# A causal mask that moves from a TensorE product to a VectorE addition, in a reordered attention pipeline

## Chip, cores and metric

The kernel runs on one core of a Trainium2 chip. The metric is the device time of one execution in microseconds, and the time of a kernel is the median over its runs. The engines are TensorE (PE in the profile; PEld is its weight load), VectorE (DVE), ScalarE (ACT), GpSimd (POOL) and SyncE (SP, which here only issues DMAs). Each engine works through its own instructions in program order and waits on semaphores for the others.

## What is computed

One transformer block on x of 8 sequences x 256 tokens x 256 features, all in float32. The change touches the attention scores; the rest is given for orientation.

```python
x = x + layernorm(attention(layernorm(x)))
x = x + layernorm(moe(layernorm(x)))

def attention(x):                       # 16 query heads, 4 key/value heads, D = 128
    q, k, v = split(x @ w_qkv.T)
    q, k = rope(layernorm(q, qn_g, qn_b)), rope(layernorm(k, kn_g, kn_b))
    scores = q @ k.T / sqrt(128)
    scores = where(causal, -inf, scores)          # no key later than its query
    return softmax(scores) @ v @ w_o.T

# moe: 8 experts of width 176, the two best per token, and a shared expert of width 352
```

## The kernel before

The program has three stretches. First comes a start of some 30 us, in which weights and x arrive, the weights are centred (so that the layer norm over a head needs no mean) and the first projections are made; its steps stand in the program one by one, in an order written out by hand. Then comes a software pipeline of slots, one slot for each of the 8 x 12 attention units plus some for filling and draining. The last stretch, from about 600 us on, computes the experts by blocks of tokens, and does not change.

A sequence has two tiles of 128 tokens (t = 0, 1). A projection `(g, t)` yields 512 columns for one tile: g = 0 to 3 are four query heads each, 4 is the keys of the four heads, 5 is the values. A unit `(g, t, r0)` is a piece of attention for key/value head g: for t = 0 four heads with 128 keys in one unit, for t = 1 two heads with 256 keys in each of two units. [...] A sequence so has 12 projections and 12 units.

In slot s the loop calls each step once, for the unit or projection that is at that step: `multiply(s)` makes a projection, `square`, `deviation` and `power` its norm's scale (ScalarE, VectorE, POOL), `normalise(s-1)` applies it on ScalarE, `rope_cos(s-1)` and `rope_sin(s-1)` turn it on VectorE and POOL, `rope_sum(s-2)` adds, `turn_heads(s-2)` transposes on TensorE and `settle_heads(s-2)` adds the rope of the norm's offset out of PSUM. With u = s - 7, `score(u)`, `maximum(u)` and `exponential(u)` make the exponentials, `inverse(u-1)` and `weights(u-1)` divide by the sums, `turn_weights(u-2)`, `copy_weights(u-2)` and `value(u-2)` multiply with the values, and `copy_value(u-3)` stores. `outputs` multiplies with `w_o`. Steps that come once per tile (`residual`, `inner`, `turn_inner`, `route`, `rank`, `mark`, `enter` and others, started by `ends`; `prepare`, `prepared`, `turn_x`, started by `begins` at a given place of the 12) are spread over the slots. The order of the calls in the slot is the order of each engine's instructions; no scheduler changes it.

PSUM is shared by tags: `mm` (projections) two buffers, `tr` (every transpose, and the small products of route, rank and enter) two, `sc` two, `av` and `o` one each. A step that needs a buffer waits for the last reader of the tile that had it.

The mask is a bfloat16 tile with -1e30 above the diagonal and 0 elsewhere. It is added by TensorE: `score` issues a product of a bfloat16 identity `identb` with the mask into the scores' own 128-key block, and the float32 score products of that block accumulate onto it. `identb` is a copy of the float32 identity, made by VectorE at the start. In the start, `find(g)` sums a group of weights on VectorE, `centre(g)` or `centre_on_act(g)` subtracts the mean on VectorE or ScalarE, `tables(s, engine)` builds the rope tables with the norm's gains on the engine named, `gains` spreads the gains over the partitions and `turn_offsets` transposes the offsets' tables.

Of the kernel before, what the change touches and what calls it, by code (L numbers as in the profile page):

```python
# [19 lines left out]
P = 128  # L20
# [28 lines left out]
def block_kernel(  # L49
# [92 lines left out]
    for j, w in enumerate((wg, wu)):  # L142
# [14 lines left out]
    nhalf = const.tile([P, REP], F32, name="nhalf")  # L157
    nc.gpsimd.memset(nhalf, -0.5)

    identb = const.tile([P, P], BF16, name="identb")  # L160
    mask = const.tile([P, REP, P], BF16, name="mask")
    nc.gpsimd.memset(mask, 0.0)
    nc.gpsimd.affine_select(
        out=mask,
# [1 line left out]
        compare_op=ALU.is_ge,  # L166
        fill=NEG,
        base=0,
        pattern=[[0, REP], [-1, P]],
        channel_multiplier=1,  # L170
    )
    iota_e = const.tile([P, E], F32, name="iota_e")
# [56 lines left out]
    def find(g):  # L229


        heads = w_qkv[g].rearrange("p c (h d) -> p (c h) d", d=D)
        wm = small.tile([P, KC * REP], F32, tag="wm", name=f"wm_{g}")
        nc.vector.tensor_reduce(out=wm, in_=heads, axis=AX.X, op=ALU.add)
        nc.vector.tensor_scalar_mul(wm, wm, -1.0 / D)
        found[g] = heads, wm
# [130 lines left out]
    with ExitStack() as actx:  # L367
# [152 lines left out]
        def gains():  # L520

            nc.vector.tensor_scalar_mul(gb_row[:, 2:], gb_row[:, 2:], scale)
            gbp = ps_o.tile([P, 4, D], F32, tag="o", name="gbp")
            nc.tensor.matmul(
                gbp.rearrange("p n d -> p (n d)"), lhsT=ones_row,
                rhs=gb_row.rearrange("p n d -> p (n d)"), start=True, stop=True,
            )
            nc.scalar.copy(gb_all, gbp)
# [10 lines left out]
        def score(b, u):  # L539
            g, t, r0 = units[u]  # L540
            nh, w = shape(u)
            sc = ps_sc.tile([P, nh, w], F32, tag="sc", name=f"sc_{b}_{u}")

            def product(h, k, **flags):
                nc.tensor.matmul(  # L545
                    sc[:, h, k * P : (k + 1) * P],
                    lhsT=seqs[b]["qT"][g][:, r0 + h, t * P : (t + 1) * P],
                    rhs=seqs[b]["kT"][:, g, k * P : (k + 1) * P],
                    **flags,
                )  # L550

            if t == 1:
                for h in range(nh):
                    product(h, 0, start=True, stop=True)
            nc.tensor.matmul(  # L555
                sc[:, :, w - P :], lhsT=identb, rhs=mask[:, :nh, :], start=True, stop=False
            )
            for h in range(nh):
                product(h, t, start=False, stop=(h == nh - 1))
            now["sc", b, u] = sc  # L560

        def maximum(b, u):
            nh, w = shape(u)
# [222 lines left out]
        def each(f, k, n=NS):  # L786

            if 0 <= k < B * n:
                f(*divmod(k, n))
# [38 lines left out]
        with tc.manual_schedule():  # L828

            warm = ps_tr.tile([P, 4, P], F32, tag="tr", name="warm")  # L830
            for k in range(WARM):
                nc.tensor.transpose(warm[:, k % 4, :], ident, ident)
            nc.vector.tensor_copy(identb, ident)
            prepare(0, 0)
            gains()
            prepare(0, 1)
            prepared(0, 0)
            find(4)
            turn_x(0, 0)
            centre(4)  # L840
            multiply(0, 0)
            find(0)
            prepared(0, 1)
            tables("k", nc.gpsimd)
            square(0, 0)
            tables("q", nc.vector)
            multiply(0, 1)
            centre_on_act(0)
            square(0, 1)
            deviation(0, 1)  # L850
            multiply(0, 4)
            power(0, 1)
            find(1)
            turn_x(0, 1)
            square(0, 4)
            multiply(0, 2)
            multiply(0, 5)
            normalise(0, 1)
            deviation(0, 4)
            power(0, 4)  # L860
            rope_cos(0, 1)
            rope_sin(0, 1)
            normalise(0, 4)
            square(0, 2)
            rope_cos(0, 4)
            rope_sin(0, 4)
            deviation(0, 2)
            centre_on_act(1)
            turn_offsets("k")
            turn_offsets("q")  # L870
            rope_sum(0, 4)
            rope_sum(0, 1)
            turn_heads(0, 1)
            power(0, 2)
            turn_heads(0, 4)
            multiply(0, 3)
            settle_heads(0, 1)
            normalise(0, 2)
            rope_cos(0, 2)
            square(0, 5)  # L880
            deviation(0, 5)
            rope_sin(0, 2)
            multiply(0, 6)
            power(0, 5)
            settle_heads(0, 4)
            normalise(0, 5)
            square(0, 6)
            square(0, 3)
            rope_sum(0, 2)
            find(2)  # L890
            turn_heads(0, 2)
            settle_heads(0, 2)
            rope_cos(0, 5)
            rope_sin(0, 5)
            deviation(0, 6)
            power(0, 6)
            LAST = B * NS + LAG + 3
            for s in range(FIRST, LAST):
                u, j = s - LAG, s
                each(copy_value, u - 3)  # L900
                ends(s, residual, 5)
                each(inverse, u - 1)
                each(turn_weights, u - 2)
                each(copy_weights, u - 2)
                each(rope_sum, j - 2)
                each(normalise, j - 1)
                each(weights, u - 1)
                begins(s, prepare, 1, 4)
                each(score, u)
                each(maximum, u)  # L910
                park(s)
                each(rope_cos, j - 1)
                each(rope_sin, j - 1)
                each(multiply, j)
                each(turn_heads, j - 2)
                begins(s, prepare, 0, 2)
                ends(s, inner, 6)
                begins(s, turn_x, 0, 6)
                ends(s, route, 8)
                begins(s, turn_x, 1, 7)  # L920
                ends(s, turn_inner, 7)
                each(settle_heads, j - 2)
                ends(s, rank, 9)
                ends(s, gates, 8)
                ends(s, mark, 9)
                ends(s, enter, 10)
                each(square, j)
                each(deviation, j)
                ends(s, shares, 9)
                each(power, j)  # L930
                ends(s, inner_rows, 6)
                ends(s, residual_sum, 5)
                begins(s, prepared, 1, 5)
                each(exponential, u)
                centre_last(s)
                outputs(s)
                begins(s, prepared, 0, 2)
                each(value, u - 2)
                if s == B * NS:

                    wgu_sb = wpool.tile([P, KC, E * 2 * HE], F32, tag="w", name="wgu_sb")
                    for j, w in enumerate((wg, wu)):
                        for c in range(KC):
                            nc.sync.dma_start(
                                out=wgu_sb[:, c, :].rearrange("p (e g h) -> p e g h", g=2, h=HE)[
                                    :, :, j, :
                                ],
                                in_=w[c * P : (c + 1) * P, : E * HE].rearrange(
                                    "p (e h) -> p e h", h=HE
                                ),  # L950
                            )

            z = B - 1
            rank(z - 1, 1)
            mark(z - 1, 1)
            shares(z - 1, 1)
            for o in range(sum(OUTPUTS[: LAST - OUT - z * NS]), H):
                output(z, o)
            enter(z - 1, 1)
            residual(z, 0)  # L960
            residual_sum(z, 0)
            for o in range(H, 2 * H):
                output(z, o)
            inner(z, 0)
            inner_rows(z, 0)
            fill(2)
            turn_inner(z, 0)
            residual(z, 1)
            route(z, 0)
            residual_sum(z, 1)  # L970
            fill(1)
            rank(z, 0)
            inner(z, 1)
            mark(z, 0)
            inner_rows(z, 1)
            fill(2)
            enter(z, 0)
            turn_inner(z, 1)
            route(z, 1)
            fill(1)  # L980
            rank(z, 1)
            mark(z, 1)
            fill(2)
            enter(z, 1)
            for t in range(NT):
                gates(z, t)
            for t in range(NT):
                shares(z, t)
# [425 lines left out]
```

## Time and profile before

| What | Value |
|---|---|
| Median of 3 runs | 768.57 us (767.18 to 769.37) |
| Profiled execution | 768.42 us, span from first to last instruction 766.3 us |
| Mean granted TensorE clock | 0.988 |
| Slots | score products from 28.1 to 563.4 us |
| DMA, page's slices | 316 and 139 GB/s in the first two of 40, about 1 to 9 up to the middle of the slots |
| POOL rope_sin (L481) | 128 + 32 instructions, 0.72 to 1.24 us each |
| ScalarE exponentials (L576) | 256, mean 435 ns |

The page gives each engine's busy time and its share of the span; slices of the span in tenths; the chain of work that ended last; and groups of instructions by line, with tile names, shapes, count, total and mean time, and behind the second bar the time that the engine stood idle just before them and for whom. In timeline lines the first two numbers are start and length in us, and brackets give the wait ahead. [...]

### The profile page before, as it was taken

Reading aid. Unit: us, or ns where it says so; the run is one execution under the profiler, and the core shown is the slowest. Engines: PE = TensorE matmul, PEld = TensorE weight load, DVE = VectorE, ACT = ScalarE, POOL = GpSimd, SP = SyncE. Lnnn points to the kernel's source line nnn. Section 1 sums busy time; section 2 is a strip of 40 time slices with the busy share of each in tenths; the row PEclk is TensorE's granted clock in tenths of the full one; section 3 lists DMA queues with packets and bytes.
Section 4 is the critical chain, followed back from the end, with each engine's and each line's share of the span. In section 5 each row is a group of like instructions: output and inputs, shape, how many; then the busy total and the mean of one; then the engine's idle time right before and its main releaser. Section 6 shows DMA issues by size and latency. Waiting matters only on the chain.

```text
span 766.3 us, 11943 instructions
## 1 busy us (share of the span) xinstructions
PE 736.0 (96%) x3800; PEld 553.1 (72%) x3800; DVE 498.5 (65%) x1372; ACT 458.0 (60%) x1448; POOL 395.0 (52%) x455
## 2 busy tenths in 40 slices
PE   7799999999999999999999999999999899999994
PEld 4457777777777777777777777777887677777774
DVE  7767657677676867776776778567546563353564
ACT  3678877576677757676776777576651333333332
POOL 6656667265555627473654556275312434455423
PEclk9899999999999999999999999999999999999998
DMA  9400000000000000000000000000403133343422
GB/s 316 139 1 1 1 1 9 0 8 2 8 1 9 0 8 8 1 8 0 9 1 8 1 7 4 5 8 23 137 9 89 42 104 111 104 125 104 122 84 75
DMA packets 26917, 32.40 MB, mean 42 GB/s; under 512 B 2980, under 2 KB 23048, under 8 KB 26856
## 3 DMA queue, kind: packets, MB, share of 16 engines
q1 hardware_dynamic: 22752, 21.94, 8.8%
q0 software_dynamic: 3408, 9.31, 4.5%
q8 instruction: 31, 0.51, 0.3%
q10 hardware_dynamic: 696, 0.40, 0.2%
q14 instruction: 30, 0.25, 0.1%
HBM read 22.33 MB, written 9.31 MB: 41 GB/s over the span
## 4 chain that ended last, share of the span: by engine, by line
PE 88%; DVE 4%; ACT 3%; DMA 2%; issue 1%; POOL 1%; DVEq 0%; POOLq 0%; ACTq 0%
PE qkv L413 20%; PE o L644 15%; PE sc L545 11%; PE av L625 10%; PE gu L1167 6%; PE tp L607 5%; PE py L1192 5%; PE tq L508 4%; PE gus L285 4%; PE sd L305 2%; PE sc L555 2%; PE xt L1150 1%; PE ht L1182 1%; PE in L773 1%; DMA w_qkv<-in_wqkvT 1%
## 5 line engine op out<-in xcount | busy, mean ns | idle before, releaser
L413 PE MATMUL qkv<-w_qkv,xnT 128*128 128x512 f32 x384 | 184.5, 604 | 3.7 <-DVE xnT L403 3.1
L481 POOL TENSOR_TENSOR t<-qn,sg_q 128x256 f32<-128x256 f32 x128 | 118.9, 948 | 58.6 <-ACT qn L455 58.6
L446 POOL TENSOR_TENSOR rstds<-ves,nhalf 128x4 f32<-128x4 f32 x80 | 84.7, 1059 | 108.9 <-DVE ves L437 54.2
L644 PE MATMUL o<-wo_sb,oT 128*128 128x256 f32 x512 | 125.1, 384 | 0.0
L545 PE MATMUL sc<-kT,q 128*128 128x128 f32 x768 | 109.4, 277 | 3.5 <-DVE q L518 3.5
L455 ACT ACTIVATE qn<-qkv,rstds 128x128 f32<-128x128 f32 x320 | 91.8, 373 | 31.3 <-POOL rstds L446 30.4
L576 ACT ACTIVATE ex<-sc,nmx 128x128 f32<-128x128 f32 (+1 forms) x256 | 105.5, 435 | 2.2 <-DVE nmx L565 1.8
L413 PEld LDWEIGHTS qkv<-w_qkv,xnT 128*128 128x128 f32 x384 | 66.8, 194 | 54.7 <-issue 48.0
L545 PEld LDWEIGHTS sc<-kT,q 128*128 128x128 f32 x768 | 101.7, 193 | 5.7 <-ACT ex L576 3.7
L625 PE MATMUL av<-pT,v 128*128 128x256 f32 (+1 forms) x320 | 98.5, 422 | 0.2 <-ACT pT L612 0.2
L644 PEld LDWEIGHTS o<-wo_sb,oT 128*128 128x128 f32 x512 | 91.4, 190 | 9.3
L565 DVE TENSOR_REDUCE nmx<-sc 128x2 f32<-128x512 f32 (+1 forms) x96 | 66.2, 690 | 48.8 <-PE sc L545 47.1
L612 ACT COPY pT<-tp 128x512 f32<-128x512 f32 x96 | 57.3, 597 | 26.1 <-PE tp L607 26.1
L508 PEld LDWEIGHTS tq<-ident,t 128*128 128x128 f32 x320 | 39.9, 142 | 43.6 <-issue 37.1
L607 PEld LDWEIGHTS tp<-ident,ex 128*128 128x128 f32 x384 | 47.6, 141 | 24.9 <-ACT sq L431 7.9
L625 PEld LDWEIGHTS av<-pT,v 128*128 128x128 f32 x320 | 59.0, 190 | 8.5 <-issue 1.0
L469 DVE TENSOR_TENSOR t<-qn,cg_q 128x512 f32<-128x512 f32 x64 | 44.6, 697 | 25.0 <-ACT qn L455 24.5
L596 ACT ACTIVATE ex<-ex,rr 128x256 f32<-128x256 f32 x128 | 59.2, 525 | 0.1
L431 ACT ACTIVATE sq<-qkv 128x512 f32<-128x512 f32 x80 | 48.2, 602 | 17.9 <-PE qkv L413 12.3
L607 PE MATMUL tp<-ident,ex 128*128 128x128 f32 x384 | 57.9, 273 | 0.7 <-DVE xnT L403 0.5
L437 DVE TENSOR_REDUCE ves<-sq 128x4 f32<-128x516 f32 x80 | 54.6, 682 | 5.5 <-ACT sq L431 5.5
L1140 POOL DMA_INDIRECT xb<-xf_rows,src x39 | 37.5, 961 | 37.7 <-PE xt L1150 20.7
(202 smaller groups left out, 1216.3 us busy)
## 6 DMA issues: line engine op xcount, KB each, us to landing
ys<-yb SPq DMA_DIRECT2D x39, 128.0 KB
w_qkv<-in_wqkvT SPq DMA_DIRECT2D x6, 512.0 KB
x_all<-in_x SPq DMA_DIRECT2D x8, 256.0 KB
wo_sb<-in_woT SPq DMA_DIRECT2D x1, 2048.0 KB
xf_rows<-xf SPq DMA_DIRECT2D x16, 128.0 KB
out<-yo SPq DMA_DIRECT2D x14, 128.0 KB
wgu_sb<-in_wg SPq DMA_DIRECT2D x2, 704.0 KB
wgu_sb<-in_wu SPq DMA_DIRECT2D x2, 704.0 KB
```

The lines of the kernel that those rows point to most:

```text
L413: nc.tensor.matmul(ps.rearrange("p h d -> p (h d)"), lhsT=seqs[b]["xnT"][t][:, c, :], rhs=w_qkv[g][:, c, :], start=(c == 0), stop=(c == KC ...
L446: nc.gpsimd.tensor_tensor(rstd, now.pop(("ve", b, j)), nhalf, ALU.pow)
L455: nc.scalar.activation(qn[:, h, :], ps[:, h, :], AF.Copy, scale=rstd[:, h : h + 1])
L481: nc.gpsimd.tensor_tensor(t2[:, :, lo : lo + HD], qn[:, :, hi : hi + HD], sg[s][:, t : t + 1, lo : lo + HD].to_broadcast([P, REP, HD]), AL ...
L508: nc.tensor.transpose(tr[:, h, :], t1[:, h, :], ident)
L545: nc.tensor.matmul(sc[:, h, k * P : (k + 1) * P], lhsT=seqs[b]["qT"][g][:, r0 + h, t * P : (t + 1) * P], rhs=seqs[b]["kT"][:, g, k * P : ( ...
L565: nc.vector.tensor_reduce(out=nm, in_=now["sc", b, u], axis=AX.X, op=ALU.max, negate=True)
L576: nc.scalar.activation(ex[:, h, :], sc[:, h, :], AF.Exp, bias=nm[:, h : h + 1], accum_out=rs[:, h : h + 1],)
L596: nc.scalar.activation(ex[:, h, :], ex[:, h, :], AF.Copy, scale=rr[:, h : h + 1])
L607: nc.tensor.transpose(tr[:, c, :], ex[:, h, k * P : (k + 1) * P], ident)
L625: nc.tensor.matmul(now["av"][:, r0 : r0 + nh, :].rearrange("p h q -> p (h q)"), lhsT=seqs[b]["v"][:, k, g * D : (g + 1) * D], rhs=pT[:, k ...
L644: nc.tensor.matmul(now["o", b, t], lhsT=seqs[b]["oT"][h // REP, t][:, h % REP, :], rhs=wo_sb[:, h, :], start=(h == 0), stop=(h == H - 1),)
```

## The change

The product with the identity goes, and `identb` with it. The score products of a unit then stand alone, each with start and stop. A new step `masked(u)` adds the mask to the scores' own block in PSUM, in place, by VectorE; the mask keeps one copy of its 128 x 128 instead of four and is spread over the heads by the access pattern. `masked` is called between `score` and `maximum`. The calls in the slot and the steps of the start stand in another order. In the slot, among others: `park` and `rope_sum` come first, `copy_value` follows `turn_weights`, `normalise` follows `score`, `inverse` comes after `rope_sum`, `square` comes before `turn_heads`, `mark` and `shares` come at the end, `centre_last` ahead of `exponential`, and `turn_x(…, 0)` moves from place 6 to place 7. In the start, both tiles of x are turned before `gains`, `centre(4)` follows `find(0)`, and `tables("q")` follows `find(1)`.

```diff
--- before.py
+++ after.py
@@ -157,8 +157,7 @@
     nhalf = const.tile([P, REP], F32, name="nhalf")
     nc.gpsimd.memset(nhalf, -0.5)
 
-    identb = const.tile([P, P], BF16, name="identb")
-    mask = const.tile([P, REP, P], BF16, name="mask")
+    mask = const.tile([P, P], BF16, name="mask")
     nc.gpsimd.memset(mask, 0.0)
     nc.gpsimd.affine_select(
         out=mask,
@@ -166,7 +165,7 @@
         compare_op=ALU.is_ge,
         fill=NEG,
         base=0,
-        pattern=[[0, REP], [-1, P]],
+        pattern=[[-1, P]],
         channel_multiplier=1,
     )
     iota_e = const.tile([P, E], F32, name="iota_e")
@@ -541,23 +540,21 @@
             nh, w = shape(u)
             sc = ps_sc.tile([P, nh, w], F32, tag="sc", name=f"sc_{b}_{u}")
 
-            def product(h, k, **flags):
-                nc.tensor.matmul(
-                    sc[:, h, k * P : (k + 1) * P],
-                    lhsT=seqs[b]["qT"][g][:, r0 + h, t * P : (t + 1) * P],
-                    rhs=seqs[b]["kT"][:, g, k * P : (k + 1) * P],
-                    **flags,
-                )
-
-            if t == 1:
+            for k in range(t + 1):
                 for h in range(nh):
-                    product(h, 0, start=True, stop=True)
-            nc.tensor.matmul(
-                sc[:, :, w - P :], lhsT=identb, rhs=mask[:, :nh, :], start=True, stop=False
-            )
-            for h in range(nh):
-                product(h, t, start=False, stop=(h == nh - 1))
+                    nc.tensor.matmul(
+                        sc[:, h, k * P : (k + 1) * P],
+                        lhsT=seqs[b]["qT"][g][:, r0 + h, t * P : (t + 1) * P],
+                        rhs=seqs[b]["kT"][:, g, k * P : (k + 1) * P],
+                        start=True,
+                        stop=True,
+                    )
             now["sc", b, u] = sc
+
+        def masked(b, u):
+            nh, w = shape(u)
+            own = now["sc", b, u][:, :, w - P :]
+            nc.vector.tensor_add(own, own, mask[:, None, :].to_broadcast([P, nh, P]))
 
         def maximum(b, u):
             nh, w = shape(u)
@@ -830,112 +827,112 @@
             warm = ps_tr.tile([P, 4, P], F32, tag="tr", name="warm")
             for k in range(WARM):
                 nc.tensor.transpose(warm[:, k % 4, :], ident, ident)
-            nc.vector.tensor_copy(identb, ident)
             prepare(0, 0)
-            gains()
             prepare(0, 1)
             prepared(0, 0)
             find(4)
+            prepared(0, 1)
             turn_x(0, 0)
-            centre(4)
+            turn_x(0, 1)
+            gains()
             multiply(0, 0)
             find(0)
-            prepared(0, 1)
+            centre(4)
             tables("k", nc.gpsimd)
-            square(0, 0)
-            tables("q", nc.vector)
+            centre_on_act(0)
             multiply(0, 1)
-            centre_on_act(0)
+            multiply(0, 2)
+            multiply(0, 4)
             square(0, 1)
             deviation(0, 1)
-            multiply(0, 4)
             power(0, 1)
             find(1)
-            turn_x(0, 1)
+            tables("q", nc.vector)
             square(0, 4)
-            multiply(0, 2)
             multiply(0, 5)
+            square(0, 0)
             normalise(0, 1)
             deviation(0, 4)
             power(0, 4)
             rope_cos(0, 1)
-            rope_sin(0, 1)
             normalise(0, 4)
             square(0, 2)
+            deviation(0, 2)
             rope_cos(0, 4)
+            rope_sin(0, 1)
             rope_sin(0, 4)
-            deviation(0, 2)
+            power(0, 2)
             centre_on_act(1)
             turn_offsets("k")
             turn_offsets("q")
-            rope_sum(0, 4)
             rope_sum(0, 1)
             turn_heads(0, 1)
-            power(0, 2)
+            rope_sum(0, 4)
+            square(0, 5)
             turn_heads(0, 4)
+            settle_heads(0, 4)
+            settle_heads(0, 1)
+            deviation(0, 5)
             multiply(0, 3)
-            settle_heads(0, 1)
+            multiply(0, 6)
             normalise(0, 2)
+            square(0, 3)
             rope_cos(0, 2)
-            square(0, 5)
-            deviation(0, 5)
             rope_sin(0, 2)
-            multiply(0, 6)
             power(0, 5)
-            settle_heads(0, 4)
+            rope_sum(0, 2)
+            find(2)
             normalise(0, 5)
             square(0, 6)
-            square(0, 3)
-            rope_sum(0, 2)
-            find(2)
             turn_heads(0, 2)
-            settle_heads(0, 2)
             rope_cos(0, 5)
             rope_sin(0, 5)
             deviation(0, 6)
             power(0, 6)
+            settle_heads(0, 2)
             LAST = B * NS + LAG + 3
             for s in range(FIRST, LAST):
                 u, j = s - LAG, s
+                park(s)
+                each(rope_sum, j - 2)
+                each(turn_weights, u - 2)
+                ends(s, residual, 5)
                 each(copy_value, u - 3)
-                ends(s, residual, 5)
+                each(copy_weights, u - 2)
+                each(score, u)
+                each(normalise, j - 1)
                 each(inverse, u - 1)
-                each(turn_weights, u - 2)
-                each(copy_weights, u - 2)
-                each(rope_sum, j - 2)
-                each(normalise, j - 1)
+                each(masked, u)
                 each(weights, u - 1)
-                begins(s, prepare, 1, 4)
-                each(score, u)
+                begins(s, turn_x, 1, 7)
+                begins(s, prepare, 0, 2)
                 each(maximum, u)
-                park(s)
                 each(rope_cos, j - 1)
                 each(rope_sin, j - 1)
                 each(multiply, j)
+                each(square, j)
                 each(turn_heads, j - 2)
-                begins(s, prepare, 0, 2)
                 ends(s, inner, 6)
-                begins(s, turn_x, 0, 6)
+                begins(s, turn_x, 0, 7)
+                ends(s, turn_inner, 7)
                 ends(s, route, 8)
-                begins(s, turn_x, 1, 7)
-                ends(s, turn_inner, 7)
+                begins(s, prepare, 1, 4)
                 each(settle_heads, j - 2)
+                ends(s, gates, 8)
+                ends(s, inner_rows, 6)
                 ends(s, rank, 9)
-                ends(s, gates, 8)
-                ends(s, mark, 9)
+                each(deviation, j)
+                centre_last(s)
                 ends(s, enter, 10)
-                each(square, j)
-                each(deviation, j)
-                ends(s, shares, 9)
                 each(power, j)
-                ends(s, inner_rows, 6)
                 ends(s, residual_sum, 5)
+                begins(s, prepared, 0, 2)
                 begins(s, prepared, 1, 5)
                 each(exponential, u)
-                centre_last(s)
                 outputs(s)
-                begins(s, prepared, 0, 2)
                 each(value, u - 2)
+                ends(s, mark, 9)
+                ends(s, shares, 9)
                 if s == B * NS:
 
                     wgu_sb = wpool.tile([P, KC, E * 2 * HE], F32, tag="w", name="wgu_sb")
```

## Prediction

> **What bounds the kernel now.** I read the page's sums and slices first, then the busy times by stretch, then the list of waits, the groups of the lines that change, and last the timeline of some slots and of the start.
>
> ```profile
> PE 736.0 (96%) x3800; PEld 553.1 (72%) x3800; DVE 498.5 (65%) x1372; ACT 458.0 (60%) x1448; POOL 395.0 (52%) x455
> PEclk9899999999999999999999999999999999999998
> 66.00:300.00 234.00, 234.00 (x1257) 174.63 (x1256) 161.76 (x423) 166.44 (x537) 130.35 (x141) 1.00 0.01 4
> 300.00:560.00 260.00, 259.93 (x1427) 198.72 (x1426) 181.27 (x509) 179.71 (x585) 136.92 (x149) 1.00 0.05 16
> ```
>
> The first two lines are of the page, the other two of the busy times by stretch (length, then PE, PEld, DVE, ACT, POOL). From 66 to 560 us TensorE is busy in 493.93 of 494 us at full clock, and the list of waits for that time holds no row of a matmul. So in the 88 slots of that stretch nothing but TensorE's own work sets the pace: 5.61 us a slot, in which VectorE is busy 3.90 us (343.0 / 88) and ScalarE 3.93. The idle TensorE has lies elsewhere: in the start (up to about 58 us), around 560 to 605 us, and in the expert stage, which the change leaves as it is.
>
> ```profile
> L555 PE MATMUL sc<-mask,identb 128*128 128x256 bf16 x64 | 17.6, 275 | 0.0
> L555 PE MATMUL sc<-mask,identb 128*128 128x512 bf16 x32 | 12.1, 379 | 0.0
> 303.64 0.61 PE L545 MATMUL sc<-kT,q 128*128 128x128 f32 x4
> 304.09 0.27 PE L555 MATMUL sc<-mask,identb 128*128 128x256 bf16 x1
> 304.20 0.61 PE L545 MATMUL sc<-kT,q 128*128 128x128 f32 x4
> 315.81 0.38 PE L555 MATMUL sc<-mask,identb 128*128 128x512 bf16 x1
> 316.03 1.05 PE L545 MATMUL sc<-kT,q 128*128 128x128 f32 x8
> ```
>
> The groups give 29.7 us for the 96 mask products, but a matmul's record runs on while the next one streams. What a product costs is the distance from its start to the next start: 0.11 us for the narrow form (304.09 to 304.20), 0.22 us for the wide one (315.81 to 316.03). The 0.10 us weight load of identb is not extra: four score products before it take 0.45 us (303.64 to 304.09), as the four after it do.
>
> **What is removed.** 96 products: 32 x 0.22 + 64 x 0.11 = 14.1 us at most; the page's chain has 2% for L555, its view in order of time 1.7% (13.0 us). I take 13.65 us (the start distances before rounding, 0.107 and 0.213, from the 0.445 us of four 128-column products). In the start some of it lies in time in which TensorE waits anyway; that is inside the start's sum below. The bf16 identity (one 2.42 us cast on VectorE from 1.50 us) goes too; the row statistics that follow begin at 3.50, when x lands, so it is worth nothing.
>
> **What is added.** 96 VectorE additions, read from PSUM and written back there. The trace has no VectorE write to PSUM. Nearest row: settle_heads (L518), PSUM in with an SBUF operand, 685 ns for 512 elements, 0.60 us from start to start when the next op is independent; for 256 elements the xnT copy out of PSUM (L403), 419 ns and 0.33 us. Sum: 32 x 0.60 + 64 x 0.33 = 40.3 us. Bounds: if the write into PSUM were free of the row's tail, no less than the elements' share of these rows, 0.27 us per 256 (0.60 - 0.33), 35 us; if the maximum, which depends on the sum, waits for the whole record, 0.72 and 0.45 us, 52 us. I take 40.3, by the nearest row. Per slot that is 0.42 us (0.54 at the upper end), so VectorE goes from 3.90 to 4.32 us in a slot that shrinks to 5.47 us: 79%, at the upper end 81%. It is hidden as long as no TensorE instruction comes to wait for something behind it on VectorE. ScalarE's exponential starts later by one addition, but it also stands behind square, which waits for the projection 1.72 us after the scores, so the addition and the maximum (0.42 + 0.69) end first.
>
> **What is moved in the slot.** TensorE's own order stays: turn_weights, score, multiply, turn_heads, the occasional turns and outputs, value. VectorE's is now rope_sum, inverse, masked, maximum, rope_cos, settle_heads, deviation. Who would be late next? A turn waits for one of two PSUM buffers (tag "tr"): the next slot's turn_weights needs settle_heads done. The tightest place is the slot with route:
>
> ```profile
> 310.82 0.69 DVE L565 TENSOR_REDUCE nmx<-sc 128x2 f32<-128x512 f32 x1 [1.02 <-PE sc L545]
> 311.54 0.69 DVE L469 TENSOR_TENSOR t<-qn,cg_q 128x512 f32<-128x512 f32 x1
> 313.32 0.17 DVE L693 MAX8 m<-r 128x8 f32<-128x8 f32 x1 [1.09 <-PE r L684]
> 314.44 0.68 DVE L518 TENSOR_TENSOR q<-tq,bbT_q 128x512 f32<-128x512 f32 x1
> 315.38 0.60 PE L607 MATMUL tp<-ident,ex 128*128 128x128 f32 x4
> ```
>
> settle_heads ends at 315.12 and turn_weights starts at 315.38: 0.2 us of slack. But VectorE sits idle 1.09 us for TensorE's r ahead of it, so the addition (0.33 us, in front of the 310.82 line) is absorbed there, and both ends of the slack move with TensorE. In the slot with rank, mark moves behind deviation, and mark and shares to the slot's end: rank 1.39, deviation 0.6, mark 0.91, shares 0.47 us, counted from settle_heads, finish about 2.4 us into the next slot; rope_sum 0.6 more, while turn_heads needs it at 3.05 us. That slot's settle_heads then ends about 0.6 us ahead of the next turn. Slots with turn_x: batch tile 0 goes from place 6 to place 7, so two turns share a slot; the old order paid there (settle_heads and deviation behind the xnT copy), and power and normalise come 0.7 us earlier. DMAs keep their order on SP (xf rows leave once per tile as before); on POOL the order within a slot stays, and the mask's set-up is a quarter of its size. I cost all this at +0.3 us, bounds -0.3 and +4 (0.25 us at each of the 16 rank slots).
>
> **The start.** Here TensorE does wait, so order counts.
>
> ```profile
> 23.28 1.07 PE L508 MATMUL tq<-ident,t 128*128 128x128 f32 x8 [0.47 <-ACT bbT_q L534]
> 31.93 0.63 PE L508 MATMUL tq<-ident,t 128*128 128x128 f32 x4 [0.85 <-DVE t L493]
> 36.04 1.19 PE L545 MATMUL sc<-kT,q 128*128 128x128 f32 x4 [3.48 <-DVE q L518]
> 38.09 3.62 PE L413 MATMUL qkv<-w_qkv,xnT 128*128 128x512 f32 x4
> ```
>
> Walked by hand in the new order, with the rows' durations: (1) centre(4) now follows find(0), which the weights' DMA holds to 9.79: 9.79 + 1.21 + 0.17 + 1.22 = 12.4 (before 9.43), so multiply(0,1) starts there; multiply(0,2), (0,4), (0,5) follow without a gap to 19.3. (2) tables("q"), 3.1 us of VectorE, used to sit in a hole at 11.60; now it follows deviation(0,1) and find(1): 16.9 to 20.0. deviation(0,4) behind it starts at 20.0, before 16.84. (3) power 1.0, normalise 1.1, square 0.5, then centre_on_act(1) 2.4 us: the offset tables leave ScalarE at 26.4 and the first head turns run from 26.2 instead of 23.28, after a gap from 20.4. (4) From there the new order gains: two projections and the first scores run straight on, the second scores wait for q until about 37.8 (36.04 before), the next projection for centre_on_act(2) (now ahead of the first exponential) until 39.3 (38.09). (5) centre_on_act(3), ahead of exponential(2), puts copy_weights(1) to 52.6; the slots then start at 54.3, 58.9 and 63.3, where they were 53.75, 58.24 and 62.69. So TensorE enters the full stretch 0.6 us later though 0.88 us of products are already gone: the start costs +1.5 us. Such a walk is good to about 2.5 us either way, and to 6 us if two delays meet.
>
> [...] The trace: after 3.48 us of waiting the projection at 38.09 takes 3.41 us to the next start (41.50), where it takes 1.72 in the slots, and the granted clock from 30 to 40 us is 0.76. [...]
>
> **Sum.** 768.42 (profiled execution, 0.15 under the median of 768.57) - 13.65 + 1.5 + 0.3 = 756.6 us, 1.6% faster.
>
> **The rivals.** (a) VectorE takes the bound, the slower side: in every slot settle_heads, and with it the next turn_weights, slips by the addition. Place: the "tr" buffers. It decides from 0.14 us a slot on (13.65 / 96). With the whole addition exposed: 756.6 + 40.3 = 797 us; with half of it, 777. For it: 0.2 us of slack in the route slots, VectorE near 80%. Against: the idle 1.0 us for PE sc and 1.09 for r, which VectorE has ahead of just these instructions. (b) The start slips more, cold clock and two delays met: +4 to +8, 760 to 765 us. For it: step (2), 3 us late on a path with no slack, and the 2.4 us blocks of ScalarE. (c) The start gets shorter, the 3.48 us wait and its cold projection being avoided: 752 to 754. For it: step (4). (d) That the change removes nothing: the instruction order of the new kernel has no product with the mask, so no.
>
> **How the numbers follow.** Forecast, 754 to 760 us: 0.66. Longer start or a few slot stalls, 760 to 766: 0.16. Shorter start, 751.5 to 754: 0.10. VectorE as the bound or stalls that outweigh the products: 0.06. Within 0.3% (2.3 us, about what a measurement of this kernel can tell from no change), a partial form of (a): 0.02. Faster by over 0.3% is then 0.92. The range 752 to 764 leaves out about a fifth of (c), a quarter of (b) and all of (a).
>
> **What would show it.** Right: no L555; TensorE busy near 722 us; still no matmul row in the waits of the middle stretch; slots of 5.47 us; VectorE near 545 us (498.5 + 32 x 0.69 + 64 x 0.42 - 2.4); an addition of about 0.68 and 0.42 us; first head turns near 26 us. Wrong: "PE tp <- DVE q" or "PE tq <- DVE t" rows with tens of entries; additions much above 0.7 us; PEclk below 9 after the first two slices; a full stretch that begins more than 4 us later than before.

## Result: 1.5% faster, and the profile after

| | before | after |
|---|---|---|
| Median of 4 runs, us | 768.33 (767.18 to 769.37) | 756.84 (755.74 to 759.31) |
| Ratio, 95% interval | 1 | 0.9855 (0.9827 to 0.9883) |
| Profiled execution, span, us | 768.42, 766.3 | 756.90, 755.2 |
| turn_weights of unit slot 4 starts, us | 62.69 | 63.21 |
| turn_weights of unit slot 84 starts, us | 518.12 | 507.77 |
| turn_weights of unit slot 93 starts, us | 562.11 | 550.22 |

The 96 units are numbered 0 to 95 here ("unit slot"), and the start of a unit's turn_weights serves as a clock for the slots, since this step stands in both kernels. From unit slot 4 to 84 the pipeline is undisturbed.

The page's sums and granted clock of the kernel after, then its busy times by stretch (length, then PE, PEld, DVE, ACT, POOL; the granted clock is the third number from the end):

```profile
PE 721.8 (96%) x3704; PEld 542.3 (72%) x3704; DVE 548.7 (73%) x1467; ACT 459.7 (61%) x1448; POOL 396.8 (53%) x455
PEclk9899999999999999999999999999999999999997
...
66.00:300.00 234.00, 233.94 (x1246) 173.87 (x1245) 191.37 (x478) 172.09 (x554) 134.93 (x146) 1.00 0.01 4
300.00:550.00 250.00, 250.00 (x1360) 190.71 (x1358) 202.97 (x546) 178.44 (x575) 134.71 (x146) 1.00 0.05 16
```

TensorE has 96 instructions fewer and VectorE 95 more (96 additions, less the cast of identb). TensorE is still busy in all of the middle (483.94 of 484 us). VectorE is busy in 394.3 of 484 us there, 81%, where it was 70%; TensorE does not pay for that yet.

The groups of the addition, shapes apart, and the timeline of VectorE and TensorE in a slot with route, the place that the prediction called the tightest:

```profile
L557 DVE TENSOR_TENSOR sc<-sc,mask 128x256 f32<-128x256 f32 x64 | 27.3, 427 | 32.3 <-PE sc L545 32.2
L557 DVE TENSOR_TENSOR sc<-sc,mask 128x512 f32<-128x512 f32 x32 | 22.0, 689 | 12.4 <-PE sc L545 12.1 <-PE rank L728 0.3
```

```profile
305.54 0.43 DVE L557 TENSOR_TENSOR sc<-sc,mask 128x256 f32<-128x256 f32 x1 [1.10 <-PE sc L545]
306.01 0.69 DVE L562 TENSOR_REDUCE nmx<-sc 128x2 f32<-128x512 f32 x1
306.62 1.14 DVE L468 TENSOR_TENSOR t<-qn,cg_q 128x512 f32<-128x512 f32 x1
308.05 0.17 DVE L690 MAX8 m<-r 128x8 f32<-128x8 f32 x1 [0.29 <-PE r L681]
309.17 0.68 DVE L517 TENSOR_TENSOR q<-tq,bbT_q 128x512 f32<-128x512 f32 x1
...
310.10 0.60 PE L604 MATMUL tp<-ident,ex 128*128 128x128 f32 x4
```

The addition sits where VectorE waits for the scores anyway: the 1.10 us wait now stands ahead of L557 instead of the maximum. Further down, the wait for r shrinks from 1.09 to 0.29 us. That is what the addition and a longer rope_cos (1.14 us, of which more below) have used up. settle_heads (L517) still ends 0.25 us before the next turn_weights at 310.10, as it did before (315.12 and 315.38).

The list of waits has no row of a matmul from 66 to 550 us. The two longest waits of a matmul in the whole run are in the start, as this timeline of TensorE shows:

```profile
25.89 1.97 PE L507 MATMUL tq<-ident,t 128*128 128x128 f32 x8 [5.01 <-ACT bbT_k L533]
27.66 4.98 PE L412 MATMUL qkv<-w_qkv,xnT 128*128 128x512 f32 x8
32.48 0.60 PE L507 MATMUL tq<-ident,t 128*128 128x128 f32 x4
...
38.60 1.13 PE L545 MATMUL sc<-kT,q 128*128 128x128 f32 x8 [2.47 <-DVE q L517]
39.56 1.88 PE L412 MATMUL qkv<-w_qkv,xnT 128*128 128x512 f32 x4
41.28 0.60 PE L507 MATMUL tq<-ident,t 128*128 128x128 f32 x4
...
63.21 0.86 PE L604 MATMUL tp<-ident,ex 128*128 128x128 f32 x4
```

The first head turns (25.89) wait 5 us for the offset tables, and the eight products of the two projections behind them take 4.82 us from start to start (27.66 to 32.48). Before, the same eight took 3.44 us (24.18 to 27.62):

```profile
24.18 3.60 PE L413 MATMUL qkv<-w_qkv,xnT 128*128 128x512 f32 x8
27.62 0.63 PE L508 MATMUL tq<-ident,t 128*128 128x128 f32 x4
```

### The profile page after: what moved, and what is told of

It is laid out like the page before. It is cut to its first block, busy times and chain, and to the rows that moved or that the text cites. A ratio compares the mean times of both kernels' runs of the same rounds, so it can differ in the third digit from the quotient of the medians.

```text
span 755.2 us, 11877 instructions
## 1 busy us (share of the span) xinstructions
PE 721.8 (96%) x3704; PEld 542.3 (72%) x3704; DVE 548.7 (73%) x1467; ACT 459.7 (61%) x1448; POOL 396.8 (53%) x455
## 4 chain that ended last, share of the span: by engine, by line
PE 87%; DVE 4%; ACT 4%; POOL 2%; DMA 2%; issue 1%; POOLq 0%; ACTq 0%; DVEq 0%
PE qkv L412 19%; PE o L641 15%; PE sc L545 11%; PE av L622 10%; PE gu L1164 6%; PE tp L604 5%; PE py L1189 5%; PE gus L284 4%; PE tq L507 4%; PE sd L304 2%; PE xt L1147 1%; PE ht L1179 1%; ACT qn L454 1%; PE in L770 1%; DMA w_qkv<-in_wqkvT 1%
## 5 line engine op out<-in xcount | busy, mean ns | idle before, releaser
L445 POOL TENSOR_TENSOR rstds<-ves,nhalf 128x4 f32<-128x4 f32 x80 | 93.6, 1170 | 75.4 <-DVE ves L436 74.9
L545 PE MATMUL sc<-kT,q 128*128 128x128 f32 x768 | 101.5, 275 | 2.5 <-DVE q L517 2.5
L545 PEld LDWEIGHTS sc<-kT,q 128*128 128x128 f32 x768 | 93.3, 192 | 2.7 <-ACT w_qkv L247 2.7
L557 DVE TENSOR_TENSOR sc<-sc,mask 128x256 f32<-128x256 f32 (+1 forms) x96 | 49.4, 514 | 44.8 <-PE sc L545 44.4
L468 DVE TENSOR_TENSOR t<-qn,cg_q 128x512 f32<-128x512 f32 x64 | 57.1, 893 | 8.0 <-ACT qn L454 7.6
L633 ACT COPY oT<-av 128x512 f32<-128x512 f32 x64 | 37.8, 590 | 35.9 <-PE av L622 35.9
```

Source lines behind the costliest of these rows:

```text
L445: nc.gpsimd.tensor_tensor(rstd, now.pop(("ve", b, j)), nhalf, ALU.pow)
L545: nc.tensor.matmul(sc[:, h, k * P : (k + 1) * P], lhsT=seqs[b]["qT"][g][:, r0 + h, t * P : (t + 1) * P], rhs=seqs[b]["kT"][:, g, k * P : ( ...
```

## The experiments

Each kernel is compared with the kernel before on the same chip, because the kernel before itself takes 768.5 us on some chips and 763 to 764 us on others. In the profiles at hand that difference lies in the expert stage: from its `total` product to the end it takes 163.1 to 163.5 us on the chips with 763 to 764 us, and 167.6 to 169.3 us on those with 768.5.

**1. The mask alone.** Mask tile, `score` and `masked` as in the change; the start and the slots' order as before.

```diff
 # before.py, with the new mask tile, score and masked; no identb
                 each(score, u)
+                each(masked, u)
                 each(maximum, u)
```

> The old order of slot and start, with only the mask moved to VectorE. Theory (products are worth what TensorE spends on them, the addition is hidden by VectorE's idle time, the new start costs about 1.5 us): 768.4 - 13.65 = 754.8 us, up to 1 us more for additions in the start; no matmul row in the waits from 66 to 550 us. Rival (the additions only fit because the slot was reordered): TensorE waits for settle_heads in the slots, 760 us or more.

Measured: 751.90 us against 763.58, ratio 0.9846 (0.9830 to 0.9863). Unit slots 4 to 84 take 444.38 us, against 455.43 before and 444.56 in the full change. So the whole gain is the mask's move, and the addition needs no new order to be hidden: VectorE has room for it in the old one as well.

**2. The order alone.** The new order of slots and start, with the mask still a product.

```diff
 # after.py, with the mask tile, identb and score of before
                 each(inverse, u - 1)
-                each(masked, u)
                 each(weights, u - 1)
```

> The new order of slot and start, with the mask still added by the TensorE product. Theory: the start costs 1.5 us, the slots nothing: 770 us (768.4 + 1.5). Rival (the reordered slot itself brings part of the gain): below 767 us.

Measured: 764.86 us against 763.58, ratio 1.0018 (1.0011 to 1.0026), which is 1.3 us slower. Slots 4 to 84 take 455.67 us, 0.24 more than before. In the slots the reordering is worth nothing; in the whole, it costs. Where, the trace does not show: the 20 runs spread from 763.39 to 766.23 us, and the profiled one is among the shortest (763.41), with unit slot 4 at 62.89, 0.2 us behind the kernel before.

**3. No mask at all.** The kernel after without the addition, so that the scores of later keys count in the softmax.

```diff
-                each(masked, u)
```

> The changed kernel without the addition; it leaves the causal mask out altogether. Theory (the 96 additions are hidden but for those in the start): 756 to 757 us, the same as with them within 1 us. Rival (VectorE is close to setting the pace and the additions cost part of the gain): 753 us or less.

Measured: 753.21 us against 763.58, ratio 0.9857 (0.9838 to 0.9875), beside 0.9855 with the addition. Slots 4 to 84 take 444.56 us, with it and without it. The addition costs 0.00 us there, although the 96 records of it sum to 49.4 us.

**4. and 8. Two and three additions.** If one is free, where does VectorE begin to set the pace? Here the mask is added two and three times (-2e30 and -3e30, still no weight).

```diff
                 each(masked, u)
+                each(masked, u)
+                each(masked, u)      # in the kernel with three
```

> The changed kernel with the mask added twice, so 96 more VectorE additions of 0.33 and 0.60 us (+40 us of VectorE, about 4.8 us busy per slot of 5.47). Theory (a slot has about 1 us of VectorE time to spare): 757 to 760 us, a little more in the start and in the slots with rank. Rival (VectorE is at its limit already): 780 us or more, with TensorE waiting for settle_heads in most slots.

> The changed kernel with the mask added three times: 80 us more of VectorE, some 5.2 us busy in a slot of 5.47. Theory (TensorE loses only what VectorE cannot fit, and with two additions it lost 0.3 us per sequence, at the slots with rank): the rank and enter slots overflow for good, 10 to 20 us over the changed kernel, with TensorE waiting for rope_sum and settle_heads. Rival (slack is spread so that a third addition is hidden as the second was): under 5 us more.

Measured: two, 758.11 us against 763.58, ratio 0.9931 (0.9915 to 0.9948); three, 793.81 us against 768.54, ratio 1.0327 (1.0296 to 1.0357). The slots 4 to 84 tell it most cleanly:

| additions | slots 4 to 84, us | added by the last one, us | VectorE busy, 66 to 550 us |
|---|---|---|---|
| 0 | 444.56 | | 72% |
| 1 | 444.56 | 0.00 | 81% |
| 2 | 446.99 | 2.43 | 88% |
| 3 | 470.43 | 23.44 | 93% |

Busy times by stretch of the kernel with two additions, then of the kernel with three, then the latter's list of waits of matmuls in this stretch (us in total, times, longest; not all its rows):

```profile
66.00:300.00 234.00, 233.92 (x1236) 172.28 (x1236) 206.78 (x515) 173.20 (x558) 133.43 (x145) 1.00 0.01 4
300.00:550.00 250.00, 249.61 (x1350) 188.55 (x1349) 218.12 (x580) 176.99 (x566) 135.00 (x146) 1.00 0.06 17
```

```profile
66.00:300.00 234.00, 226.03 (x1175) 162.51 (x1174) 217.44 (x529) 163.74 (x525) 117.73 (x135) 1.00 0.01 4
300.00:550.00 250.00, 240.79 (x1263) 175.76 (x1262) 232.58 (x591) 171.22 (x549) 122.45 (x147) 1.00 0.02 5
```

```profile
PE sc L545 <- DVE q L517: 6.0, 7, 1.1
PE tx L400 <- DVE xnT L402: 3.1, 6, 0.6
PE tq L507 <- DVE rr L581: 2.7, 7, 0.5
PE tq L507 <- DVE t L492: 2.0, 5, 0.4
```

With three, TensorE waits for VectorE: at settle_heads (q), rope_sum (t) and the copy of the turned tokens (xnT), and VectorE sets the pace in some of the slots. Not in all: in the fourth sequence seven of the twelve slots keep the length that they have with one addition, to 0.03 us. The other five grow by 0.10, 0.35, 0.65, 1.00 and 1.98 us. The 1.98 (6.08 to 8.06) are in the slot with both copies of xnT, the 1.00 (6.52 to 7.52) in one with the hot and share steps that follow rank. So the place of the loss was forecast in part (the slots behind rank), but its size was too low, at 10 to 20 us: against the kernel after on the same chip it is 36.8 us (793.81 and 757.03), of which some 26 lie in slots 4 to 84 and the rest in the start, the draining and behind. Three additions on one block stand in the timeline as one row of 1.34 us (narrow) or 2.14 us (wide), so each further one takes half of what is above the single 0.43 and 0.69 us: 0.46 and 0.73 us. For 80 units that makes about 44 us (53.3 x 0.46 + 26.7 x 0.73), of which 23.4 are paid.

**5. The kernel after again**, beside the next ones: 757.03 us against 768.54, ratio 0.9848 (0.9824 to 0.9873), unit slot 4 at 63.49.

> The changed kernel once more, as the measure for the starts sent with it. Both theories: 0.9855 of the kernel before; unit slot 4's turn_weights near 63.2 to 64.9 us.

**6. The old start with the changed slots.** The one-by-one calls from `prepare(0, 0)` to the loop are those of before; the diff is the start's part of the change, backwards.

```diff
+            centre(4)
             multiply(0, 0)
             find(0)
-            centre(4)
...
+            tables("q", nc.vector)
             multiply(0, 1)
...
             find(1)
-            tables("q", nc.vector)
```

> The changed slot with the start of the kernel before. Theory (the new start costs about 1.5 us and the slots do not depend on it): 1 to 1.5 us less than the changed kernel, with unit slot 4's turn_weights near 62 us. Rival (start and slot order belong together, the first slots lose what the start gains): the same as the changed kernel.

Measured: 754.71 us against 768.54, ratio 0.9815 (0.9791 to 0.9839): 2.3 us less than the kernel after, and all five runs (754.19 to 755.22) lie under all five of its neighbour on the same chip (kernel 5, 756.51 to 758.21). The first head turns start at 23.35 (26.16 in the neighbour), unit slot 4 at 60.20, 3.3 us earlier than there (63.49). I had given the start 1 to 1.5 us. It costs 2.3 to 3.3, and the new order of the first slots seems to hide part of that: with the old start on both sides, slot 4 comes at 60.20 with the new slots, where the old ones give 61.81 (62.69 less 0.88 us of products) or, measured in kernel 1, 62.53. So 1.6 to 2.3 us come back, but from single executions: in kernel 1 the eight products behind the first head turns took 4.68 us, in kernel 6 3.43, behind waits of the same length (2.16 and 2.15 us), so that up to 1.25 us of it may be chance.

**7. Three calls of the new start put right.** The calls behind steps (1) and (2) of the prediction's walk put back, and multiply(0,4) with them; the rest of the start kept.

```diff
             multiply(0, 0)
-            find(0)
             centre(4)
+            find(0)
+            tables("q", nc.vector)
             tables("k", nc.gpsimd)
...
             multiply(0, 1)
-            multiply(0, 2)
             multiply(0, 4)
+            multiply(0, 2)
...
             find(1)
-            tables("q", nc.vector)
```

> The changed kernel with three moves in its start: centre(4) ahead of find(0), tables(q) into VectorE's hole right behind find(0), multiply(0,4) ahead of multiply(0,2). Theory (step 2 of the forecast: deviation(0,4), late behind find(1), tables(q) and the projection of j = 2, holds the chain to the first head turns): the first head turns about 2 us earlier, near 24 us, and the slots 1 to 1.5 us earlier. Rival (the later waits for centre_on_act(2) and (3) on ScalarE set the start's end anyway): head turns earlier, but the slots within 0.4 us of the changed kernel's.

Measured: 755.09 us against 768.54, ratio 0.9822 (0.9797 to 0.9847). TensorE's timeline:

```profile
23.54 1.45 PE L507 MATMUL tq<-ident,t 128*128 128x128 f32 x8 [3.07 <-ACT bbT_k L533]
24.78 5.05 PE L412 MATMUL qkv<-w_qkv,xnT 128*128 128x512 f32 x8
29.67 0.60 PE L507 MATMUL tq<-ident,t 128*128 128x128 f32 x4
```

The first head turns come at 23.54, and unit slot 4 at 60.40: about all of what the old start gives. All five runs (754.52 to 756.13) lie under those of kernel 5. So the three calls that were moved here, centre(4) behind find(0), tables("q") behind find(1) and multiply(0,4) behind multiply(0,2), carry nearly all of the start's cost; which of them how much was not run. The eight products still take 4.89 us.

**9. TensorE kept busy.** Is it the gap that makes the eight products behind it slow, at a lower granted clock? 48 transposes whose result nobody reads, behind `turn_offsets("q")` in the kernel after.

```diff
             turn_offsets("q")
+            warm = ps_sc.tile([P, 4, P], F32, tag="sc", name="warm_2")
+            for k in range(48):
+                nc.tensor.transpose(warm[:, k % 4, :], ident, ident)
             rope_sum(0, 1)
```

> The changed kernel with 48 idle transposes on TensorE behind turn_offsets, in the gap from about 20.5 to 26 us, so that the clock is not lowered. They compute nothing that is used. [...] Rival (ScalarE's and POOL's chain through normalise and power sets the start's end, TensorE is not on it): projections faster, slots within 0.3 us of the changed kernel's (63.2 to 63.5 us for unit slot 4).

Measured: 751.02 us against 764.09, ratio 0.9836 (0.9821 to 0.9851); the interval overlaps that of the kernel after, so the time alone does not decide. The busy times by stretch of the kernel after, then of this one, and TensorE's timeline of this one do:

```profile
20.00:30.00 10.00, 4.99 (x17) 3.14 (x15) 6.03 (x10) 6.90 (x24) 6.64 (x9) 0.68 0.79 248
```

```profile
20.00:30.00 10.00, 10.00 (x69) 7.85 (x67) 6.80 (x11) 7.18 (x24) 7.75 (x9) 1.00 0.78 244
```

```profile
20.42 5.40 PE L870 MATMUL warm<-ident 128*128 128x128 f32 x48
26.53 3.60 PE L412 MATMUL qkv<-w_qkv,xnT 128*128 128x512 f32 x8
...
37.43 2.05 PE L545 MATMUL sc<-kT,q 128*128 128x128 f32 x8 [2.57 <-DVE q L517]
39.27 2.50 PE L412 MATMUL qkv<-w_qkv,xnT 128*128 128x512 f32 x4
```

From 20 to 30 us the granted clock is 1.00 instead of 0.68. With the gap filled the eight products take 3.60 us instead of 4.98, and unit slot 4 starts at 62.05, 1.2 us earlier than the 63.21 of the kernel after (0.3 of them stand ahead of the added work, as `turn_offsets("q")` runs at 20.20 for 20.50). The gap made them slow: behind the same gap of 5.0 us they took 3.96 to 5.27 us from start to start in all six profiles that have it, and 3.80 in the one where it is filled. So the length of the gap alone did not fix what it cost. But the next gap (2.57 us ahead of the second scores) is now followed by slower work: the scores take 2.05 us (1.13 in the kernel after), the projection 2.50 (1.88), and the granted clock from 30 to 40 us is 0.86 (0.98 in the kernel after).

**10. and 11. A start without the gap.** Kernel 7 with the offset turns ahead of centre_on_act(1) (10), and that with 28 idle transposes (11).

```diff
+            turn_offsets("k")
+            turn_offsets("q")
+            # in 11 alone: 28 transposes into a "sc" tile, as in 9
             centre_on_act(1)
-            turn_offsets("k")
-            turn_offsets("q")
```

> The start with the three moves, and turn_offsets ahead of centre_on_act(1), so that the offset tables' copies do not stand behind 2.4 us of ScalarE. Theory (after the three moves rope_sum of j = 4 is ready only 0.3 us before the tables): the first head turns 0.3 us earlier, slots 0 to 0.3 us earlier than with the three moves, about 755 us. Rival (the copies are what holds the path): 1 to 2 us earlier.

> The start of the run before (three moves, offsets ahead of centre_on_act(1)) with 28 idle transposes, 3.1 us, in the gap that is left there. Theory (the two projections behind the gap are on the path, as the warm clock showed by 1.2 to 1.4 us in the changed kernel): unit slot 4 about 1.2 us earlier, near 59.3 us; the time about 0.9800 of the kernel before. Rival (with the shorter gap the other engines' chain sets the start's end): slots within 0.3 us of 60.5.

Measured: 10, 749.33 us against 764.09, ratio 0.9814 (0.9801 to 0.9828); 11, 749.99 against 763.11, ratio 0.9822 (0.9809 to 0.9835). Kernel 10 has its head turns at 23.63 and slot 4 at 60.55, the same as kernel 7: the wait passes from the tables to VectorE's t. Kernel 11 misses its forecast (slot 4 at 62.96, not 59.3). Two rows of it, the busy times of an early stretch (granted clock third from the end) and a projection of its timeline:

```profile
10.00:20.00 10.00, 10.00 (x18) 4.25 (x18) 8.07 (x13) 5.31 (x15) 5.48 (x9) 0.72 1.07 363
...
38.90 3.62 PE L412 MATMUL qkv<-w_qkv,xnT 128*128 128x512 f32 x4
```

Its clock was already down to 0.72 ahead of the added work, in which kernel 10 has 0.83, and the turns of the offsets stood 1.53 us later than there (21.55 and 20.02). So 1.5 of the 2.4 us by which slot 4 is late were lost ahead of what was added. Behind it the two projections took 3.60 us for the 4.79 of kernel 10, but the four products at 38.90 took double their usual 1.88. Whether that was its own order or the chance of one execution, the run does not say; that filling this gap pays in total stays open.

Kernels 6 and 10 are the fastest. Both beat the kernel before by 1.85% and stand at 0.9815 and 0.9814 beside the 0.9855 of the change, though the intervals touch (0.9827 to 0.9883 for the change).

## Why the prediction held, step by step

**Products removed (13.65 us).** Right. For the 80 units between slots 4 and 84 the start-to-start distances make 13.65 x 80 / 96 = 11.4 us. Measured, new order with and without products: 455.67 - 444.56 = 11.11; old order: 455.43 - 444.38 = 11.05. The records of the groups (29.7 us for 96) would have doubled the forecast. The 0.107 and 0.213 us of the forecast were an estimate; in the trace of before the medians from start to start are 0.109 and 0.215 us, 13.9 us for the 96.

**Addition hidden (0).** Right: 0.00 us by kernel 3. The records are as forecast from the PSUM reads: 427 and 689 ns, for 0.42 and 0.68. But the price of 40.3 us, which took an independent operation to follow, was too low: in the middle stretch the maximum mostly follows, which depends on the addition, and starts 0.46 or 0.73 us after it. That is the prediction's upper bound (52 us), and VectorE's share its upper 81%. It cost nothing, since the cover was wide enough for it. With a second addition (88% of VectorE's time) the cover begins to wear, with a third (93%) it is gone in five of twelve slots. Rival (a) is thus real as a mechanism and two additions away as a case.

**Slots' order and tail (+0.3).** About nothing, within the bounds: 0.18 us from slot 4 to 84 (444.56 against 444.38 with the old order), 0.24 with the products; counted to slot 93 the new order is even 0.30 and 0.14 us shorter. Of the spans' difference, 11.17 us, slots 4 to 93 give 12.41 less, the start takes back 0.52 net of its own removed products, and the stretch behind the slots 0.72 (0.41 up to the `total` product of the expert stage, which kernel 1 with the old order has as well, and 0.31 behind it).

**The start (+1.5).** The sum was right: slot 4 came 0.52 later, with 0.88 us of products gone, so +1.4. And the walk met its points: head turns 25.89 (forecast 26.2), second scores 38.60 (37.8), slot 4 at 63.21 (63.3). But I took 1.5 us for the price of the new start, and that is where a term was mis-sized. Step (4), "from there the new order gains", hid a second one: the start costs 2.3 to 3.3 us (kernel 6), and the slots' new order returns some of it, 1.6 to 2.3 by single executions. That the two together made 1.4 is in part luck. Rival (c), a shorter start, falls by kernel 6, and rival (b), 4 to 8 us longer, was not reached.

**The slow work behind the gap.** How much of the +1.5 stood for slow work behind the new gap was an estimate of mine, and no run shows that share. The traces show this in its place: behind a gap of 5.0 us the eight products took 4.82 us, at a granted clock of 0.71, for 3.44 at 1.00 before, 1.4 us more, and kernel 9 took most of that away (3.80). But the walk left out the other side: the projection that was slow before (3.41 us from 38.09, at 0.50) took 1.72 in the kernel after (39.56 to 41.28, at 1.00), behind a wait of 2.47 us for 3.48. So the slow work changed places more than it grew. Nor did the length of the wait tell which work would be slow: products were slow behind waits of 3.07 us (4.89, kernel 7) and 2.16 us (4.68, kernel 1), and not behind 2.15 us (3.43, kernel 6).

**VectorE's busy time (545).** It came to 548.7. The groups of rope_cos show where the rest is, first of the kernel after, then of before:

```profile
L468 DVE TENSOR_TENSOR t<-qn,cg_q 128x512 f32<-128x512 f32 x64 | 57.1, 893 | 8.0 <-ACT qn L454 7.6
```

```profile
L469 DVE TENSOR_TENSOR t<-qn,cg_q 128x512 f32<-128x512 f32 x64 | 44.6, 697 | 25.0 <-ACT qn L455 24.5
```

That is 196 ns more for each of 64, 12.5 us of records. The new order alone brings 58 of them: the mean is 755 ns in kernels 2 and 3, which have that order and no addition. The addition brings the rest: behind it rope_cos starts later, and in 28 of 70 cases from 66 to 550 us POOL's rope_sin has already begun (the last section has the lines). The engine's busy time grew by less (3.6 us over the forecast's sum); neighbouring records overlap at their ends (the maximum above ends at 306.70, rope_cos begins at 306.62), but the remainder I did not trace. No TensorE instruction waits for it in the slots. The forecast had not looked at what POOL does when VectorE's instruction moves.

## What to carry to other kernels

Price a removed matmul by the distance to the next start on TensorE, not by its record (here 11.1 us came back in slots 4 to 84, where the distances gave 11.4 and the records 24.8); price an added VectorE operation by asking whether it stands in a wait that the engine has anyway, then by what the engine has to do in the fullest slots. The mean share is only a first hint: here the addition was free at 81%, and at 93% seven of twelve slots still hid all three. When a diff brings a new order along, run the two halves apart: the order of the slots was worth nothing and three misplaced calls of the start took 2 us of the gain. In a start written out by hand, each call that stands behind a transfer or another engine's long block should be followed to the first TensorE instruction that needs it.

## What the runs showed that I had not expected

- The pace of the slots repeats far better than the time: slots 4 to 84 of the kernel after took 444.56 and 444.57 us in two profiles, and 444.54 to 444.57 in all seven profiles of kernels with these slots, on several chips, while the start varied by up to 1.7 us (unit slot 4 at 64.89 in kernel 3, which has less to do, and at 63.21 in the kernel after) and the whole by 5 us between chips. A fixed stretch between two records tells differences that the medians cannot.
- VectorE's rope_cos and POOL's rope_sin take longer where one begins inside the other. In the slot shown above POOL's rope_sin had begun 0.14 us before rope_cos:

```profile
306.48 1.86 POOL L480 TENSOR_TENSOR t<-qn,sg_q 128x256 f32<-128x256 f32 x2 [1.85 <-ACT qn L454]
```

and rope_cos took 1.14 us. In the next slot rope_cos began first, at 313.12 (POOL at 313.23), and took 0.69 us:

```profile
313.12 0.69 DVE L468 TENSOR_TENSOR t<-qn,cg_q 128x512 f32<-128x512 f32 x1
```

So rope_cos took 0.45 us more where it came second. Of rope_sin's two instructions the one that began inside rope_cos took 1.17 us in both slots, the other 0.73, which makes the 1.86 us. Over the whole kernel after, the 76 instructions of rope_sin that begin inside a rope_cos took 1.16 us on the mean, the other 84 took 0.73 us on the mean. In the kernel with three additions, where rope_cos came only after it, rope_sin took 1.41 us:

```profile
306.72 1.41 POOL L480 TENSOR_TENSOR t<-qn,sg_q 128x256 f32<-128x256 f32 x2
```

No addition overlaps a rope_sin in the kernel after from 66 to 550 us, so whether that would lengthen its 427 and 689 ns is not shown. Who begins first follows the addition: from 66 to 550 us rope_cos began first in all 70 cases of the kernel before (mean 0.69 us) and of kernels 2 and 3 (0.74 us), which have no addition; with the addition ahead of it, it began inside a running rope_sin in 28 of 70 in the kernel after, and took 1.11 us there on the mean, against 0.71 in the other 42. No experiment moved rope_sin itself, so the cause of the longer times is not shown.
- With a gap on TensorE filled at one place, slow work turned up at another (one execution each): behind the next gap of 2.57 us the scores took 2.05 us in kernels 9 and 11, where they take 1.13 in the kernel after, and the projection behind them 2.50 and 3.62, for 1.88. So I would price a filled gap by all that follows it.
